# Tiles, latents and weights in two shared buffers, one transpose per tile, and a dense layer in two parts

## The chip, the cores and the metric

The kernel runs on one core of one Trainium2 chip. The metric is the device time of one execution in microseconds (us): the median of several runs of the same program. The core has five engines that work beside each other, each through its own instructions in order: TensorE (PE) multiplies matrices and adds into eight banks of PSUM; VectorE (DVE), ScalarE (ACT) and GpSimd (POOL) work element by element, POOL on SBUF only; SyncE (SP) issues transfers, among them the transposes by DMA. Engines wait for each other by semaphores only.

## The reference, cut to what matters

Two layers over x of shape (2, 1024, 512), two batches of 1024 tokens:

```python
xn = layernorm(x)
x = x + attn0(xn) + streams0(xn)      # one head of 128; four streams mixed by a Sinkhorn matrix
xn = layernorm(x)
x = x + attn1(xn) + ffn1(xn)

# attn1: 32 causal query heads of 128, 8 key/value heads out of latents
lat = concat(xn @ Wk_down.T, xn @ Wv_down.T, per head)   # 512 columns
k, v = (first half of lat) @ Wk_up.T, (second half) @ Wv_up.T
out = softmax(q @ k.T * scale + causal) @ v, then @ Wo.T

# ffn1: a dense layer and a low-rank part weighted by a gate
gates = relu(layernorm(xn @ gw1.T + gb1)) @ gw2.T + gb2
top 2 of 8 experts, softmax of the two -> top_g
allowed = (tokens of each expert, over BOTH batches, <= capacity)
w = top_g where allowed, else 0                          # combine weights
out = xn @ weight.T + ((xn @ lora_A) * w) @ lora_B / 16
```

The combine weights of batch 0 need the gates of batch 1 too, since tokens are counted over both.

## The kernel before

Every fp32 operand of a product is split into two fp16 parts, high and low, and a product is three passes (high-high, high-low, low-high), added up in PSUM; `mm3` (line 84) does that. A weight is loaded in fp32 and split by three POOL instructions (`split_pool`, line 93: scale, cast, subtract). A product is brought out of PSUM by `evac` (line 104): ACT writes the high part, DVE the low part.

A tile is 128 tokens; a batch has eight. `normed_T` (line 228) makes a tile of xn for the products: it scales the tile (on DVE, POOL or ACT), casts it (ACT), subtracts (DVE or POOL) and has SP transpose both parts by DMA into a destination. `layernorm_tiles` (line 215) makes the statistics on DVE.

After layer 0 (lines 996 to 1049) layer 1 runs as one loop over 16 groups of four query heads, eight groups per batch, each of 32 steps (`layer1_attn`, line 785). A step computes the scores of 32 query rows of four heads against the keys so far (`row_step`, line 339), the softmax of the step before, and the transposes of its probabilities. A step at the start of a group is short and one at its end is long, since the attention is causal. All else hangs on steps: `at` and `put` enter a function at a step (an absolute number, 32 per group), and it is called when the loop comes there. So group 6 is steps 192 to 223, group 7, the last of batch 0, is 224 to 255, and group 14 is 448 to 479. What is entered:

- for the next group: keys and values (`kv`, line 712: load, split, two key products, two value products), query products, output weights
- for the group itself: probabilities times values (`av`), the output product (`wo_block`, line 751), which adds to the residual `acc` and, in a batch's last group, sends the tile out
- for batch 1's layer 0: Sinkhorn on POOL (steps 1 to 116), mixing (122 to 193)
- batch 1's second layer norm in one piece, `late_norm` (step LN1 = 198)
- gating: `gating_h` (the product with gw1) and the steps of `gating` (line 893, DVE throughout); batch 0 from step G0 = 16, batch 1 from G1 = 200
- `weights_of` (line 943) at WT = 220: one product with ones counts the experts' tokens over both batches, DVE makes the combine weights of both
- the dense layer of batch 0: `ffn_fetch` and `ffn_split` for six 256 KB weights (A to D dense, E and F low-rank) from FW = 210, `ffn_block` (line 975) from FF = 221; of batch 1 from step 464 and 483
- batch 1's tiles from LX = 231, its latents from LA = 240, its first keys from step 243

The scheduler that builds the program simulates it and orders each engine's instructions by what is ready, so functions of neighbouring steps mix.

Two buffers of 16 KB per partition hold the large things. `xT` (one buffer) holds the transposed tiles: layer 0 of batch 0, of batch 1, then layer 1 of batch 0 and of batch 1. `cmp` (one buffer) holds layer 0's weights, batch 0's latents, its six dense weights, batch 1's latents, its dense weights. Batch 1's tiles can't enter `xT` before batch 0's dense layer and last query products have read it (step 231), but its gating is needed before. So `tile_of` (line 1033) makes each of batch 1's tiles a first time, into a small buffer, for the gating alone (steps 200 to 207), and `xT_tile` makes it again at step 231 and later.

`ffn_block` computes the low-rank product (128 columns), multiplies it by the combine weights (`tw`, DVE), splits it (`twhl`, two DVE instructions), transposes it (`twT`, SP), and adds dense and low-rank products in one PSUM bank: 12 matmuls with A to D, then 3 with `twT` and F. PSUM has three banks for such products (`pp`), four for scores, one for `av`.

Of the kernel before, what the change touches and what calls it, by code (L numbers as in the profile page):

```python
# [9 lines left out]
F16 = mybir.dt.float16  # L10
F32 = mybir.dt.float32
AF = mybir.ActivationFunctionType
# [4 lines left out]
P = 128  # L17
S = 1024
NB = 2
NT = S // P  # L20
H = 512
NC = H // P
NH = 32
NG = 8
# [4 lines left out]
FB, PB, LB, XB, WB = 4, 3, 3, 4, 9  # L29
# [9 lines left out]
CA, CB, CC, CD = 4, 1, 1, 3  # L39
SK0, SKN, MX0, MXN, LN1 = 1, 116, 122, 74, 198  # L40

G0, G1, GL, WT, LX, LA = 16, 200, 3, 220, 231, 240
AVD, WOD = 5, 10
KVN, QN, QNN, QH = 19, 18, 24, 1
MG = range(8, 16)
FW, FF = 210, 221
BS, BP, BV = 4, 3, 1
CQ, CV = (0, 1), (0, 0)
PSCALE = 16384.0
# [3 lines left out]
def tile_model(ctx: ExitStack, tc: tile.TileContext, out: bass.AP, a: dict):  # L53
# [30 lines left out]
    def mm3(dst, pairs):  # L84

        n = len(pairs)
        for i, (lhs, rhs) in enumerate(pairs):
            for j, (l, r) in enumerate(PASSES):
                nc.tensor.matmul(dst, lhs(l), rhs(r),  # L89
                                 start=(i == 0 and j == 0),  # L90
                                 stop=(i == n - 1 and j == 2))
# [37 lines left out]


    load_x(0)
    w0 = T("cmp", [P, NC * 2 * S], F16, bufs=1)
    cut = [0]

    def part0(*shape):
# [79 lines left out]
    def layernorm_tiles(b, mv, rs, ts):  # L215
        ve = T("ve", [P, NT], bufs=2)
        sl = slice(ts[0], ts[-1] + 1)
        for t in ts:
            st = T("bnst", [P, 6], bufs=2)
            V.bn_stats(st, acc[b, t])  # L220
            V.bn_aggr(mv[:, t, :], st)
# [3 lines left out]
        return V.scalar_tensor_tensor(rs[:, 1, sl], mv[:, sl, 0], -1.0, rs[:, 2, sl],  # L225
                                      ALU.mult, ALU.mult)

    def normed_T(b, mv, rs, t, dst, pool, tags=(("f2k", FB), ("wo", WB))):

# [140 lines left out]

    def front0(b, between=lambda: None):
        mv, rs = layernorm(b, "a")
        xT = T("xT", [P, NT, 2 * NC, P], F16, bufs=1)
        for ts in F0[b]:
            layernorm_tiles(b, mv, rs, ts)
            for t in ts:
# [311 lines left out]
                last_lat[0] = evac(src, dst[:, :, 0, :], dst[:, :, 1, :], 0.125)  # L688

    def latents(b):  # L690
        cmp[b] = T("cmp", [P, NC, 2, S], F16, bufs=1)

    def lat_w(mc):
        st = T("f2k", [P, NC, P], bufs=FB)
# [51 lines left out]
    def qproj(b, w, Q, hh, half):  # L746

        p = proj_T(lambda c, l: w[:, l, c, :], xT1[b], half)
        evac(p.rearrange("p (b q) -> p b q", q=QR), Q[:, 0, :, hh, :], Q[:, 1, :, hh, :], 0.125)

    def wo_block(b, t, ao, wos, last):
        p = PP()
        mm3(p, [(lambda l, h=h: ao[:, l, h, :],
                 lambda r, h=h: wos[h][:, r, :]) for h in range(4)])
        V.scalar_tensor_tensor(acc[b, t], p, 1.0 / 256.0, acc[b, t], ALU.mult, ALU.add)  # L755
        if last:
            nc.scalar.dma_start(out[(b * NT + t) * P:(b * NT + t + 1) * P, :], acc[b, t])

    def group_av(Vh, Vm, PT, c, k, p):

# [24 lines left out]
    def layer1_attn(kv0, start, extra):  # L785
# [43 lines left out]
        for g in range(N):  # L829
            if g + 1 < N:  # L830
                new = (g + 1) % NG == 0
                kvs[g + 1], fs = kv((g + 1) // NG, (g + 1) % NG)
                at(g, KVN - 2 if new else 1, fs[0])
                for k, f in enumerate(fs[1:]):
                    at(g, KVN + 2 * k if new else 1 + 4 * k + 2 * (k == 0), f)
                for hh in range(4):
                    at(g, 5 + 4 * hh, lambda g=g, hh=hh: fetch_q(g + 1, hh))
                    at(g, 7 + 4 * hh, lambda g=g, hh=hh: split_q(g + 1, hh))
                for u in range(4):
                    at(g, QNN + 2 * u if new else QN + 4 * u, lambda g=g, u=u: q_unit(g + 1, u))  # L840
# [124 lines left out]
    def ffn_fetch(k):  # L965
        ffw[k] = fetch(ffw_parts[k][0])

    def ffn_split(k):
        if k == 0:
            ffw["w"] = T("cmp", [P, 6, 2, H], F16, bufs=1)  # L970
        w = ffw["w"][:, k]
        behind(split_pool(ffw[k], w[:, 0], w[:, 1], ffw_parts[k][1]), last_low[0], True)
        ffw["ABCDEF"[k]] = w

    def ffn_block(b, t):
        xT = xT1[b]
        pa = PP()
        la = ffw["E"].rearrange("p l (c d) -> p l c d", c=NC)
        mm3(pa[:, :P], [(lambda l, c=c: xT[:, t, 2 * c + l, :],
                         lambda r, c=c: la[:, r, c, :]) for c in range(NC)])  # L980
        tw = T("tw", [P, 8, 16], bufs=1)
        V.scalar_tensor_tensor(tw, pa[:, :P].rearrange("p (e r) -> p e r", r=16), 1.0 / 16.0,
                               bc(wts[b][:, t, :], 2, 16), ALU.mult, ALU.mult)
# [3 lines left out]
        nc.sync.dma_start_transpose(tT, hl.rearrange("p l d -> p (l d)"))  # L987
        p = PP()
        mm3(p, [(lambda l, c=c: xT[:, t, 2 * c + l, :],
                 lambda r, c=c: ffw["ABCD"[c]][:, r, :]) for c in range(NC)]  # L990
            + [(lambda l: tT[:, l, :], lambda r: ffw["F"][:, r, :])])
        V.scalar_tensor_tensor(acc[b, t], p, 1.0 / 256.0, acc[b, t], ALU.mult, ALU.add)


    f0, ln1 = {}, {}
# [28 lines left out]
    adv(200)  # L1024

    def new_xT(b):
        xT1[b] = T("xT", [P, NT, 2 * NC, P], F16, bufs=1)
# [34 lines left out]
    gw1 = gating_w()  # L1062
    chain = sinkhorn(1, logit[1])

    def late_norm():
        ln1[1] = layernorm(1, "b")
        layernorm_tiles(1, *ln1[1], range(NT))
# [19 lines left out]
    hs, gates, dts, lw = {}, {}, {}, {}  # L1087

    def gate_start(b):
        hs[b] = T("xr", [P, NT, 32], bufs=XB)  # L1090
# [17 lines left out]
    put(0, LX, lambda: new_xT(1))  # L1108
    for t in range(NT):
# [9 lines left out]
        for th in range(2):  # L1119
            put(0, LA + 2 * mc + th, lambda mc=mc, th=th: lat_unit(mc, th))  # L1120
    for k in range(6):
        for s in (FW, 8 * 58 + 2):
            put(0, s + 2 * k - 2, lambda k=k: ffn_fetch(k))
            put(0, s + 2 * k, lambda k=k: ffn_split(k))
# [51 lines left out]
```

## Time and profile before

| what | value |
|---|---|
| median of 3 runs | 1851.71 us (1848.24 to 1853.01) |
| the profiled execution: span from first to last instruction | 1846.2 us |
| instructions | 35059 |
| PE busy | 1708.2 us, 93% |
| DVE busy | 1473.1 us, 80% |
| ACT busy | 1191.1 us, 65% |
| POOL busy | 896.5 us, 49% |
| mean granted PE clock | 0.976 of full speed |

The execution that was profiled has no time of its own beside its span; the runs are others of the same program. The page's slices of the span, 46.2 us each, show where engines work, in tenths:

```profile
PE   4666389999999999998999999999999999999998
DVE  8888968988888878778976768778787877787675
POOL 5568629778766465647634433323242424235200
PEclk9888699999999999999999999999999999999999
```

A 9 stands for 90% or more. Layer 0 takes the first six slices, with gaps on PE; layer 1 fills the rest. The slices 18 to 22 (counted from 0, from 831 to 1062 us) are where batch 0 ends and batch 1 begins: there PE has its one 8 between slice 5 and the last, and DVE a 9 (slice 19). A matmul counts as busy from its start to a modelled end, so a busy PE isn't always PE at its peak.

### The profile page before, as it was taken

The page shows a single profiled execution, that of the slowest core. Times are in us where ns is not written, and L with a number is a line of the kernel's source. Part 1 is how long each engine was busy: PE and PEld are TensorE (multiplying, and loading weights), DVE is VectorE, ACT ScalarE, POOL GpSimd, SP SyncE. Part 2 cuts the span into 40 slices and gives each one's busy share as a digit, 9 for nine tenths or more (in the row PEclk, how much of TensorE's full clock was granted, in tenths as well). Part 3 has the DMA queues.
Part 4 walks back from the last instruction along what each step waited for, and adds up shares of the span by engine and source line. Part 5 has one row for each costly group of instructions (what it writes and reads, how often), then busy time and mean ns, then how long its engine had stood idle before and what let it go on. Part 6 is the DMA issues. An engine that isn't in the chain of part 4 may idle for free.

```text
span 1846.2 us, 35059 instructions
## 1 busy us (share of the span) xinstructions
PE 1708.2 (93%) x11394; PEld 1038.5 (56%) x11394; DVE 1473.1 (80%) x4162; ACT 1191.1 (65%) x2917; POOL 896.5 (49%) x1476
## 2 busy tenths in 40 slices
PE   4666389999999999998999999999999999999998
PEld 2434146566666566655555566666666666666565
DVE  8888968988888878778976768778787877787675
ACT  4848666656676778876544656667666767676564
POOL 5568629778766465647634433323242424235200
PEclk9888699999999999999999999999999999999999
DMA  7435225656575656468645656556566655566455
GB/s 212 82 56 132 59 44 123 151 118 139 119 149 98 141 128 144 105 142 143 146 98 125 144 126 140 135 124 141 125 134 124 142 118 142 124 143 135 97 121 118
DMA packets 693482, 230.25 MB, mean 125 GB/s; under 512 B 674081, under 2 KB 674209, under 8 KB 693298
## 3 DMA queue, kind: packets, MB, share of 16 engines
q1 hardware_dynamic: 677842, 180.75, 47.3%
q0 software_dynamic: 13152, 43.07, 8.7%
q10 hardware_dynamic: 2304, 4.20, 0.7%
q8 instruction: 89, 1.46, 0.3%
q14 instruction: 95, 0.78, 0.1%
HBM read 52.81 MB, written 4.19 MB: 31 GB/s over the span
## 4 chain that ended last, share of the span: by engine, by line
PE 47%; DVE 2%; DMA 1%; POOL 1%; issue 1%; ACT 0%; SPq 0%; DVEq 0%
PE pp L89 26%; PE av L365 11%; PE s L89 10%; DVE Phl L330 0%; DVE f2k L913 0%; DMA f2k<-in_Wq 0%; DMA xT<-wo 0%; DVE P L288 0%; POOL wo L241 0%; DMA PT<-Phl 0%; POOL f2k L95 0%; SPq L335 0%; DVE P L284 0%; DMA twT<-twhl 0%; DVE Q L106 0%
## 5 line engine op out<-in xcount | busy, mean ns | idle before, releaser
L292 ACT ACTIVATE P<-P,nm 128x1024 f32<-128x1024 f32 (+31 forms) x528 | 391.5, 742 | 280.9 <-DVE nm L284 263.4
L330 DVE SCALAR_TENSOR_TENSOR Phl<-P,r,Phl 128x64 f16<-128x64 f32 (+16 forms) x627 | 460.8, 759 | 75.7 <-ACT Phl L322 70.3
L89 PE MATMUL s<-K,Q 128*128 128x512 f16 (+22 forms) x2400 | 439.1, 317 | 19.7 <-DVE P L288 11.7
L365 PE MATMUL av<-PT,V 128*128 128x256 f16 x3456 | 425.6, 274 | 9.4 <-DMA PT<-Phl 8.5
L365 PEld LDWEIGHTS <-V 128*128 128x128 f16 x3456 | 338.2, 98 | 92.9 <-DMA PT<-Phl 10.6
L322 ACT ACTIVATE Phl<-P,r 128x1024 f16<-128x1024 f32 (+31 forms) x515 | 369.5, 730 | 20.6 <-DMA PT<-Phl 5.3
L89 PE MATMUL pp<-xT,wq 128*128 128x512 f16 x1536 | 371.8, 381 | 4.5 <-DVE Q L106 2.3
L89 PE MATMUL pp<-wo,ao 128*128 128x512 f16 x1536 | 369.9, 379 | 2.0 <-ACT ao L105 1.9
L95 POOL TENSOR_SCALAR f2k<-f2k 128x512 f32<-128x512 f32 x164 | 113.9, 695 | 500.6 <-DVE Phl L330 458.9
L89 PEld LDWEIGHTS <-Q 128*128 128x128 f16 x2400 | 222.8, 98 | 175.7 <-issue 27.7
L89 PEld LDWEIGHTS <-wq 128*128 128x128 f16 x1536 | 149.7, 98 | 172.6 <-issue 6.8
L89 PEld LDWEIGHTS <-ao 128*128 128x128 f16 x1536 | 149.5, 98 | 156.9 <-ACT ao L105 3.4
L284 DVE CUSTOM_DVE_ANT_0 P<-s,mask,nm 128x272 f32<-128x272 f32 (+15 forms) x256 | 157.3, 615 | 9.3 <-PE s L89 1.0
L288 DVE TENSOR_SCALAR_CACHE_REDUCE P<-s 128x512 f32<-128x512 f32 (+15 forms) x272 | 152.6, 562 | 13.4 <-PE s L89 11.2
L316 DVE RECIPROCAL r<-r 128x1 f32<-128x1 f32 x528 | 78.9, 154 | 87.5 <-ACT P L292 84.5
L317 ACT ACTIVATE r<-r 128x1 f32<-128x1 f32 x528 | 95.6, 192 | 60.2 <-DVE r L316 59.7
L105 ACT ACTIVATE ao<-av 128x512 f16<-128x512 f32 x128 | 74.9, 585 | 81.7 <-PE av L365 81.5
L334 POOL MEMSET Phl<- 128x192 f16 (+1 forms) x320 | 56.2, 189 | 142.3 <-DMA PT<-Phl 97.3
L105 ACT ACTIVATE Q<-pp 128x512 f16<-128x512 f32 x128 | 74.6, 583 | 64.3 <-PE pp L89 60.0
L284 DVE CUSTOM_DVE_ANT_0 P<-s,mask 128x32 f32<-128x32 f32 (+15 forms) x256 | 103.7, 430 | 14.9 <-PE s L89 14.2
L755 DVE SCALAR_TENSOR_TENSOR acc<-pp,acc 128x512 f32<-128x512 f32 x128 | 87.1, 681 | 35.1 <-PE pp L89 34.7
L106 DVE SCALAR_TENSOR_TENSOR Q<-pp,Q 128x512 f16<-128x512 f32 x128 | 87.4, 683 | 34.0 <-ACT Q L105 33.7
(256 smaller groups left out, 2153.1 us busy)
## 6 DMA issues: line engine op xcount, KB each, us to landing
f2k<-in_Wq POOLq DMA_DIRECT2D x64, 256.0 KB, 3.1
f2k<-in_WoT POOLq DMA_DIRECT2D x64, 256.0 KB, 3.3
PT<-Phl SPq DMA_TRANSPOSE x528, 3.2
acc<-in_x SPq DMA_DIRECT2D x16, 256.0 KB, 5.1
f2k<-in_Wup POOLq DMA_DIRECT2D x16, 256.0 KB, 3.3
out<-acc ACTq DMA_DIRECT2D x16, 256.0 KB, 3.5
xr<-V SPq DMA_DIRECT2D x32, 128.0 KB, 2.4
xr<-in_x SPq DMA_DIRECT2D x12, 256.0 KB, 3.9
```

The costliest lines, as they stand in the source:

```text
L89: nc.tensor.matmul(dst, lhs(l), rhs(r), start=(i == 0 and j == 0), stop=(i == n - 1 and j == 2))
L95: first = G.tensor_scalar(stage, stage, scale, 1.0, ALU.mult, ALU.mult)
L105: A.activation(hl_hi, src, AF.Copy, scale=scale)
L106: return V.scalar_tensor_tensor(hl_lo, src, scale, hl_hi, ALU.mult, ALU.subtract)
L284: last_row[0] = V.tensor_tensor_reduce(Pm[:, o:o + w], pt[:, :w], mask[:, 512 - w:], -scale, first, ALU.add, ALU.min, nm[:, k:k + 1])
L288: last_row[0] = V.tensor_scalar(Pm[:, o:o + w], pt[:, :w], -scale, first, ALU.mult, ALU.min, accum_out=nm[:, k:k + 1])
L292: A.activation(Pm[:, :W], Pm[:, :W], AF.Exp, bias=last, scale=-1.0, accum_out=r[:, 0:1])
L317: A.activation(r[:, 1:2], r[:, 1:2], AF.Copy, scale=PSCALE)
L322: A.activation(hl[1], Pm[:, :W], AF.Copy, scale=r[:, 1:2])
L330: last_low[0] = V.scalar_tensor_tensor(lo, Pm[:, a0:a1], r[:, 1:2], hi[:, a0:a1], ALU.mult, ALU.subtract)
L365: nc.tensor.matmul(p, v, pt, start=(k == 0), stop=(k == len(todo) - 1))
L755: V.scalar_tensor_tensor(acc[b, t], p, 1.0 / 256.0, acc[b, t], ALU.mult, ALU.add)
```

## The change

- `cmp` and `xT` become one tag, `big`, with two buffers of the same 16 KB. A new tile takes whichever is free.
- Batch 1's tiles are made once, into a `big` buffer, at steps LX = 217 and on; `tile_of` is gone, and `gating_h` of batch 1 reads these tiles three steps later.
- For that a buffer must be free while batch 0's tiles live. Keys and values of a batch's last group are computed earlier (KVL: steps 3, 4, 5, 7 and 8 of the group before it, not 3, 5, 9, 13 and 17; groups 6 and 14), so that the latents can go; then A to E take their buffer from step 201, and batch 1's tiles take it after them.
- Batch 0's dense layer is cut in two around the combine weights, which now come at WT = 240. `ffn_first` (from FF = 209): the low-rank product goes to an fp32 tile of its own (`lows`, by ACT), and the 12 dense matmuls are added to `acc`. `ffn_rest` (from LF = 241): the combine weights are put to the kept product, and the 3 matmuls with F, split apart into an `xr` buffer, are added to `acc` by a second DVE addition. Batch 1 keeps `ffn_block` as one piece.
- Batch 1's gating steps move from 211 to 228 and on, its latents from 240 to 232.
- The statistics of batch 1's second norm are spread over steps 198 to 205, the rest of it at 206.
- A tile of batch 0 leaves when both its output product of group 7 and `ffn_rest` are through (`missing`, `store`).

```diff
-G0, G1, GL, WT, LX, LA = 16, 200, 3, 220, 231, 240
+G0, G1, GL, WT, LX, LA = 16, 217, 3, 240, 217, 232
+LF = 241
+KVL = (3, 4, 5, 7, 8)
-FW, FF = 210, 221
+FW, FF = 201, 209
...
-    w0 = T("cmp", [P, NC * 2 * S], F16, bufs=1)
+    w0 = T("big", [P, NC * 2 * S], F16, bufs=2)
...
+    missing = {(0, t): 2 for t in range(NT)}
+    def store(b, t):
+        missing[b, t] = missing.get((b, t), 1) - 1
+        if missing[b, t] == 0:
+            nc.scalar.dma_start(out[(b * NT + t) * P:(b * NT + t + 1) * P, :], acc[b, t])
...
+                last = (g + 2) % NG == 0
                 for k, f in enumerate(fs[1:]):
-                    at(g, KVN + 2 * k if new else 1 + 4 * k + 2 * (k == 0), f)
+                    at(g, KVN + 2 * k if new else KVL[k] if last else 1 + 4 * k + 2 * (k == 0), f)
...
-    def ffn_split(k):
-        if k == 0:
-            ffw["w"] = T("cmp", [P, 6, 2, H], F16, bufs=1)
-        w = ffw["w"][:, k]
+    def ffn_split(k, apart=False):
+        if apart:
+            w = T("xr", [P, 2, H], F16, bufs=XB)
+        else:
+            if k == 0:
+                ffw["w"] = T("big", [P, 6, 2, H], F16, bufs=2)
+            w = ffw["w"][:, k]
...
+    def ffn_first(b, t):
+        lows[t] = T("ysum", [P, P], bufs=8)
+        A.activation(lows[t], ffn_low(b, t), AF.Copy, scale=1.0 / 16.0)
+        ffn_add(b, t, ffn_main(b, t))
+    def ffn_rest(b, t):
+        ffn_add(b, t, ffn_weigh(b, t, lows[t], 1.0))
+        store(b, t)
+    def ffn_block(b, t):
+        low = ffn_weigh(b, t, ffn_low(b, t), 1.0 / 16.0)
+        ffn_add(b, t, ffn_main(b, t) + low)
...
-    def tile_of(b, t):
-        d = T("wo", [P, 2 * NC, P], F16, bufs=WB)
-        normed_T(b, *ln1[b], t, d, True, (("f2k", FB), ("xr", XB)))
-        return d
...
-            if b == 0:
-                put(0, s + t, lambda t=t: gating_h(hs[0], t, gw1, xT1[0][:, t]))
-            else:
-                put(0, s + t, lambda t=t: dts.update({t: tile_of(1, t)}))
-                put(0, s + t + GL, lambda t=t: gating_h(hs[1], t, gw1, dts[t]))
+            put(0, s + t + GL * b, lambda b=b, t=t: gating_h(hs[b], t, gw1, xT1[b][:, t]))
...
-    put(0, LN1, late_norm)
+    for t in range(NT):
+        put(0, LN1 + t, lambda t=t: late_stats(t))
+    put(0, LN1 + NT, late_norm)
...
+        if k < 5:
+            put(0, FW + 2 * k - 2, lambda k=k: ffn_fetch(k))
+            put(0, FW + 2 * k, lambda k=k: ffn_split(k))
+    put(0, LF - 4, lambda: ffn_fetch(5))
+    put(0, LF - 2, lambda: ffn_split(5, True))
     for t in range(NT):
-        put(0, FF + t, lambda t=t: ffn_block(0, t))
+        put(0, FF + t, lambda t=t: ffn_first(0, t))
+        put(0, LF + t, lambda t=t: ffn_rest(0, t))
         put(60, 4 * t + 3, lambda t=t: ffn_block(1, t))
```

The new functions it calls: `ffn_low` is the low-rank product of a tile into PSUM; `ffn_weigh` puts the combine weights to it, splits and transposes it, and returns the pair of `twT` and F; `ffn_main` returns the four pairs of A to D; `ffn_add` multiplies what it is given and adds it to `acc`. `late_stats` makes one tile's statistics, `late_norm` the rest of the norm.

More of the change, by code (lines that the diff above doesn't have):

```diff
@@ L213, in layernorm, with norm_stats, norm_scales @@
         return mv, rs
-    def layernorm_tiles(b, mv, rs, ts):
+    def norm_stats(b, mv, t):
+        st = T("bnst", [P, 6], bufs=2)
+        V.bn_stats(st, acc[b, t])
+        V.bn_aggr(mv[:, t, :], st)
+    def norm_scales(mv, rs, ts):
         ve = T("ve", [P, NT], bufs=2)
         sl = slice(ts[0], ts[-1] + 1)
[L218 to L221, printed above, removed]
         V.tensor_scalar(ve[:, sl], mv[:, sl, 1], LN_EPS, None, ALU.add)
@@ L226, in layernorm_tiles @@
                                       ALU.mult, ALU.mult)
+    def layernorm_tiles(b, mv, rs, ts):
+        for t in ts:
+            norm_stats(b, mv, t)
+        return norm_scales(mv, rs, ts)
     def normed_T(b, mv, rs, t, dst, pool, tags=(("f2k", FB), ("wo", WB))):
@@ L372, in front0 @@
         mv, rs = layernorm(b, "a")
-        xT = T("xT", [P, NT, 2 * NC, P], F16, bufs=1)
+        xT = T("big", [P, NT, 2 * NC, P], F16, bufs=2)
         for ts in F0[b]:
@@ L690, in latents @@
     def latents(b):
-        cmp[b] = T("cmp", [P, NC, 2, S], F16, bufs=1)
+        cmp[b] = T("big", [P, NC, 2, S], F16, bufs=2)
     def lat_w(mc):
@@ L756, in wo_block @@
         if last:
-            nc.scalar.dma_start(out[(b * NT + t) * P:(b * NT + t + 1) * P, :], acc[b, t])
+            store(b, t)
     def group_av(Vh, Vm, PT, c, k, p):
@@ L966, in ffn_fetch, with ffn_low @@
         ffw[k] = fetch(ffw_parts[k][0])
-    def ffn_split(k):
-        if k == 0:
-            ffw["w"] = T("cmp", [P, 6, 2, H], F16, bufs=1)
-        w = ffw["w"][:, k]
+    def ffn_split(k, apart=False):
[5 more added lines that the diff above has]
+            w = ffw["w"][:, k]
         behind(split_pool(ffw[k], w[:, 0], w[:, 1], ffw_parts[k][1]), last_low[0], True)
         ffw["ABCDEF"[k]] = w
-    def ffn_block(b, t):
+    def ffn_low(b, t):
         xT = xT1[b]
@@ L980, in ffn_block, with ffn_weigh @@
                          lambda r, c=c: la[:, r, c, :]) for c in range(NC)])
+        return pa[:, :P]
+    def ffn_weigh(b, t, low, scale):
         tw = T("tw", [P, 8, 16], bufs=1)
-        V.scalar_tensor_tensor(tw, pa[:, :P].rearrange("p (e r) -> p e r", r=16), 1.0 / 16.0,
+        V.scalar_tensor_tensor(tw, low.rearrange("p (e r) -> p e r", r=16), scale,
                                bc(wts[b][:, t, :], 2, 16), ALU.mult, ALU.mult)
@@ L987, in ffn_block, with ffn_main, ffn_add @@
         nc.sync.dma_start_transpose(tT, hl.rearrange("p l d -> p (l d)"))
+        return [(lambda l: tT[:, l, :], lambda r: ffw["F"][:, r, :])]
+    def ffn_main(b, t):
+        return [(lambda l, c=c: xT1[b][:, t, 2 * c + l, :],
+                 lambda r, c=c: ffw["ABCD"[c]][:, r, :]) for c in range(NC)]
+    def ffn_add(b, t, pairs):
         p = PP()
-        mm3(p, [(lambda l, c=c: xT[:, t, 2 * c + l, :],
-                 lambda r, c=c: ffw["ABCD"[c]][:, r, :]) for c in range(NC)]
-            + [(lambda l: tT[:, l, :], lambda r: ffw["F"][:, r, :])])
+        mm3(p, pairs)
         V.scalar_tensor_tensor(acc[b, t], p, 1.0 / 256.0, acc[b, t], ALU.mult, ALU.add)
+    lows = {}
+    def ffn_first(b, t):
[4 more added lines that the diff above has]
+        ffn_add(b, t, ffn_weigh(b, t, lows[t], 1.0))
+        store(b, t)
+    def ffn_block(b, t):
+        low = ffn_weigh(b, t, ffn_low(b, t), 1.0 / 16.0)
+        ffn_add(b, t, ffn_main(b, t) + low)
     f0, ln1 = {}, {}
@@ L1026, in new_xT @@
     def new_xT(b):
-        xT1[b] = T("xT", [P, NT, 2 * NC, P], F16, bufs=1)
+        xT1[b] = T("big", [P, NT, 2 * NC, P], F16, bufs=2)
     def xT_tile(b, t, pool):
@@ L1063, in tile_model, with late_stats @@
     chain = sinkhorn(1, logit[1])
+    def late_stats(t):
+        if t == 0:
+            ln1[1] = layernorm(1, "b")
+        norm_stats(1, ln1[1][0], t)
     def late_norm():
-        ln1[1] = layernorm(1, "b")
-        layernorm_tiles(1, *ln1[1], range(NT))
+        norm_scales(*ln1[1], range(NT))
     extra = {}
@@ L1086, in tile_model @@
         put(1, 2 * t, lambda t=t: branch0_add(1, t, y4s[t], f0[1][4]))
-    hs, gates, dts, lw = {}, {}, {}, {}
+    hs, gates, lw = {}, {}, {}
     def gate_start(b):
@@ L1121, in tile_model @@
     for k in range(6):
-        for s in (FW, 8 * 58 + 2):
-            put(0, s + 2 * k - 2, lambda k=k: ffn_fetch(k))
-            put(0, s + 2 * k, lambda k=k: ffn_split(k))
+        if k < 5:
+            put(0, FW + 2 * k - 2, lambda k=k: ffn_fetch(k))
+            put(0, FW + 2 * k, lambda k=k: ffn_split(k))
+        put(58, 2 * k, lambda k=k: ffn_fetch(k))
+        put(58, 2 * k + 2, lambda k=k: ffn_split(k))
+    put(0, LF - 4, lambda: ffn_fetch(5))
+    put(0, LF - 2, lambda: ffn_split(5, True))
     for t in range(NT):
-        put(0, FF + t, lambda t=t: ffn_block(0, t))
+        put(0, FF + t, lambda t=t: ffn_first(0, t))
+        put(0, LF + t, lambda t=t: ffn_rest(0, t))
         put(60, 4 * t + 3, lambda t=t: ffn_block(1, t))
```

## The prediction

> **What bounds the kernel now.** I read the chain of waits first, then the busy time by group, then TensorE's (PE's) waits and the rows around them.
>
> ```profile
> PE 47%; DVE 2%; DMA 1%; POOL 1%; issue 1%; ACT 0%; SPq 0%; DVEq 0%
> ```
>
> The chain that ended last can be followed back to 893 us, and 47% of the span on PE is 868 of the 953 us behind that: from there on PE is the bound. The groups of layer 1 begin where the first 32-column score product appears; over four of them (5 to 8, numbered from 0):
>
> ```profile
> core 0: us, PE busy (x) PEld busy (x) DVE busy (x) ACT busy (x) POOL busy (x), PEclk, DMA share, GB/s
> 729.00:825.79 96.79, 95.66 (x630) 58.50 (x628) 75.41 (x201) 76.60 (x209) 55.89 (x81) 1.00 0.59 128
> 825.79:946.92 121.13, 108.32 (x784) 67.25 (x782) 103.72 (x277) 72.56 (x175) 82.17 (x116) 0.96 0.72 147
> 946.92:1086.15 139.23, 137.16 (x861) 78.22 (x862) 95.66 (x250) 75.54 (x183) 48.84 (x76) 1.00 0.54 123
> 1086.15:1177.40 91.25, 91.25 (x608) 56.41 (x606) 72.53 (x202) 60.79 (x149) 31.58 (x51) 1.00 0.58 133
> ```
>
> Columns: length, then PE, weight loads, VectorE (DVE), ScalarE (ACT) and GpSimd (POOL) with counts, granted clock, DMA. Group 6 is the sick one: DVE 86% and POOL 68% busy, PE not full, clock 0.96. How much is lost there follows from PE's timeline, where matmuls in a run start 0.216 us apart at 512 columns (12 in 2.59), 0.109 at 256, 0.056 at 128, 0.025 at 32. Group 6 holds 207, 261, 72 and 96 of these, and 144 score products whose widths add up to 21.5: 44.7 + 28.5 + 4.0 + 2.4 + 21.5 = 101.1 (101.2 with the two tiny ones). Group 7: 405 of 512 columns, 192 of 256, 120 of 128 and the scores, 136.6. The same sum gives groups 8 to 14 their measured lengths within 0.1, so PE has no slack there. Loss: 121.1 - 101.2 = **19.9 us in group 6, 139.2 - 136.6 = 2.6 in group 7**. Groups 1 to 5 lose 5.6, 1.4, 0.9, 1.6 and 3.5.
>
> ```profile
> 858.19 0.81 PE L89 MATMUL s<-K,Q 128*128 128x512 f16 x3
> 861.22 4.44 PE L89 MATMUL pp<-xT,wq 128*128 128x512 f16 x12 [2.22 <-DVE acc L755]
> ```
>
> ```profile
> 850.04 3.41 DVE L330 SCALAR_TENSOR_TENSOR Phl<-P,r,Phl 128x352 f16<-128x352 f32 x1
> 850.79 2.27 POOL L241 TENSOR_TENSOR xr<-f2k,xr 128x512 f16<-128x512 f32 x2
> ```
>
> PE waits 2.22 us for a DVE addition and then runs its 12 matmuls in 4.44 us, not 2.75. Ten microseconds before, a DVE low part that takes 0.82 at this width on average, this one counted in, took 3.41, beside two subtractions of batch 1's first set of tiles on POOL. Mapped onto PE's work, the 19.9 lie as 10.4 before 869 us and 9.5 between 914 and 947, where the gating of batch 1 fills DVE and the two count products and the first low-rank product follow it:
>
> ```profile
> PE pp L946 <- DVE ch L940: 1.1, 1, 1.1
> PE pp L89 <- DVE al L948: 0.7, 1, 0.7
> ```
>
> **The change, part by part.** PE runs 11394 matmuls in both; the dense layer's 15 wide products per tile are only cut into 12 and 3. So the time moves only by what PE waits, and 22.5 us is all that groups 6 and 7 have to give. In the changed order they hold 118.8 and 120.2 us of matmuls.
>
> *Shared buffers.* Layer 0's order differs only in neighbours changing places (first weights split after, not before, four scale steps). Two loads of 16 KB stay live, as before. PE is idle 107 us before 276 us, 70 of them for transposed tiles, which hang on the loads, the norms and a serial chain of 0.3 us steps on DVE; no neighbour changes their number, and a swap costs or gives a DVE row or two. I take 0, -2 to +2.
>
> *First set of tiles gone.* Removed: 8 scalings (1.01) and 8 subtractions (1.19) on POOL, 17.7 us; 8 casts on ACT (0.62), 5.0; 8 transposes on SP (issue to landing 3.8). None is on PE's path by itself; they lengthen DVE's rows and fill queues. POOL in group 6 falls from 82 to about 62 us (its last dense weight, 3.0 us of three rows, leaves too), a load near groups 4 and 5, which lose 1.6 and 3.5. The first 10.4 us become 4 (1 to 6).
>
> The Trainium skill, "SBUF — State Buffer", section "Who interferes with whom", says that a DVE instruction with two SBUF inputs and a POOL instruction that reads SBUF exclude each other for a whole instruction; the 3.41 us row agrees. By it up to 17.7 us of DVE time would come back, this part would fall to 0 and the sum below to -10.5 (1841.2). The same rule speaks against the change where POOL splits the dense weights in one run: were DVE blocked through all of it, the next part would be 8.7 in place of 2, and the sum +0.2 (1851.9).
>
> *Dense weights earlier, products in group 6.* Buffer, weights and first product form a queue: last value product of group 7; on POOL four casts and four subtractions in a row (4 x 0.77 + 4 x 1.41 = 8.7), since four weights wait for the latents' buffer; four DMA issues (4 x 0.58); a query weight's three rows (2.6); then cast and subtraction of the fifth weight (2.2): about 16 us, against some 15 us of PE work in the changed order until PE wants that weight. Behind that product on PE stand scores, and behind these the softmax rows. Cost 0 to 8.7 (all of the run of eight); I take 2. Eight ACT copies of 128 columns (0.28) replace the casts. Eight more additions on DVE (0.61 each in a run, 4.9 us) come where 17 us of gating leave (8 x 0.70, 8 x 0.41, some 8 of small rows), covered by PE. The 9.5 us go; 2 stay.
>
> *Buffer handed on twice more.* Batch 1's eight transposes go into the dense weights' buffer, so the first waits on SP for the eighth main product, and the softmax transposes behind it wait too. Some 10 us of PE work stand between that product and the first gating product that reads the tiles, against a landing of 3.3; latents need the old tiles' buffer, free after group 7's last query product, with 5 us of PE work before the first eviction. Both 0; if SP's queue eats the cover, one landing, inside the upper bound of the next part.
>
> *Gating, latents, combine weights in group 7.* Before, DVE was busy 95.7 there; with the gating it needs about 113 of PE's 120. They bunch: from the 9th to the 29th score row the changed order puts 56.7 us of matmuls on PE, and on DVE 32 score reductions (18.1), 19 low parts (15.5), 32 latent lows (11.3), 12 evictions (7.4), gating (7.7), combine weights (1.2), their products' splits (3.3), 21 reciprocals (1.8): 66.3, each row at its listed mean less the 0.07 by which consecutive rows overlap. DVE is short by 9.6. In group 6 the same count between the 17th and the 29th row was 38.7 against 30.7, short by 8, and PE lost 9.5. So I take 10 in place of 2.6; from 2.6 (four score banks and spare work at the group's end take the lag up) to 18 (all of the gating's 17 beside the old loss).
>
> *Low-rank product alone.* Three matmuls per tile now wait for a chain of three DVE rows, a transpose (landing 2.3) and SP's queue, without their own tile's 12 matmuls before them. The order gives the chain some 4 us of DVE rows between the last split and the addition that reads the product; before, 16 such blocks made PE wait 0.2. Behind a late product stand scores and output products on PE, and DVE's rows wait for these. I take 0; rival B prices the rest. Both norm parts and earlier key and value work in groups 6 and 14 move DVE rows of equal number; group 14 loses 0.0 and its like, groups 8 to 10, have DVE 78 to 80% busy, so 0.
>
> Sum: 4 + 2 + 10 = 16 in place of 22.5, **-6.5 us**. The profiled span is 1846.2, the median 1851.7 (5.5 above, for what lies around the span and the spread of runs); the span falls to 1839.7 and the median to **1845.2**. Bounds of the parts: 1 + 0 + 2.6 - 2 = 1.6 and 6 + 8.7 + 18 + 2 = 34.7, that is -20.9 and +12.2.
>
> **Rivals.**
>
> A, no change: gating merely brings its loss to group 7 (12) and the early loss stays, since group 1's 5.6 shows that POOL needs no such tiles for it (6), with 4 on the weights: 22, 1851. For it: DVE's total grows. Against: 17.7 us of POOL leave the worst place.
>
> B, slower: the three matmuls stand at PE's head until their transpose lands. SP's queue waited 16.1 us in 5 cases for these splits, once 7.6, and softmax transposes now stand between. If PE waits 2.3 (one landing) for each of 8, that is 18.4: 1863. From 0.8 each (6.5 / 8) the gain is lost. Against: the wait of 0.2 in 16 blocks, spread over less crowded DVE queues though.
>
> C, better: DVE's lag is taken up and both losses shrink to the average of groups 1 to 5 (2.6 each): 22.5 - 5.2 = 17.3, 1834. For it: 14 us of spare PE work follow in group 7. Against: PE keeps its order, and group 6 lost all that DVE was short.
>
> **How the numbers follow.** Forecast 0.45 (1840 to 1850), C 0.17, A 0.23, B 0.15. The range must reach A and part of B and C: 1833 to 1859 leaves out some 0.1 on each side. 0.3% (5.6 us) is about what a measurement can tell from no change: faster means below 1846.1, slower above 1857.3. Faster 0.17 + 0.31 of the forecast's 0.45 + 0.02 of A = 0.50; slower 0.13 of B and 0.03 of A = 0.16; the rest 0.34.
>
> **What would show it.** Group 6 near 125 us (118.8 + 6) with no DVE low part above 3 us in its first half; a PE wait for the fifth dense weight's POOL rows of 0 to 3 us; group 7 near 130 with DVE above 90% in its middle and PE waiting there for DVE rows; groups 8 to 14 unchanged. Wrong if PE waits repeatedly for the combine transposes (B), if group 7 has no PE wait (C), or if time up to 270 us moves by more than 2.

## The result, and the profile after

The changed kernel takes 1865.1 us (median of 6 runs, 1861.9 to 1870.0) against 1852.4 for the kernel before (6 runs beside them): ratio 1.0073, 95% interval 1.0056 to 1.0090. It is slower by some 13 us (12.7 between the medians, 13.5 by the ratio), where -6.5 was forecast. The profiled spans are 1861.8 and 1846.2, a difference of 15.6.

First the chain that ended last, and the slices of the span, from the page of the changed kernel:

```profile
PE 40%; DVE 2%; DMA 1%; issue 1%; ACT 0%; SPq 0%; DVEq 0%; ACTq 0%; POOL 0%; POOLq 0%
```

```profile
PE   4766389999999999999999799999999999999998
DVE  7988968988888877778579847878787877777675
```

The slices are 46.5 us each. PE's share of the chain has gone from 47% (868 us) to 40% (745 us): the stretch before the end in which PE's own work sets the pace is shorter. PE's weak slice inside layer 1 is slice 22, a 7 (counted from 0: 1024 to 1070 us), late in group 7; DVE has a 9 just before it, an 8 in it and a 4 behind it.

Where the 15.6 us lie follows from the first 32-column score of each group, read off PE's timeline in both traces:

| stretch | before | after | difference |
|---|---|---|---|
| up to group 0 | 263.7 | 266.9 | +3.2 |
| groups 0 to 5 | 562.1 | 562.1 | 0.0 |
| group 6 | 121.1 | 126.3 | +5.2 |
| group 7 | 139.2 | 145.5 | +6.3 |
| groups 8 and 9 | 183.2 | 182.1 | -1.1 |
| groups 10 to 13 | 363.7 | 363.7 | 0.0 |
| group 14 to the last output product | 206.2 | 208.4 | +2.2 |

Set against PE's matmuls, which the change moves between groups, group 6 loses 126.3 - 118.8 = 7.5 and group 7 145.5 - 120.2 = 25.3; together 32.8 in place of 22.5. The two groups in windows (columns as in the prediction):

```profile
829.00:955.30 126.30, 120.14 (x863) 73.50 (x862) 88.39 (x218) 70.31 (x173) 61.16 (x91) 1.00 0.60 118
955.30:1100.80 145.50, 128.75 (x796) 72.46 (x794) 115.71 (x320) 79.96 (x189) 54.06 (x90) 0.95 0.59 129
```

Group 6 is better, as forecast: DVE at 70% in place of 86%, the clock at 1.00, 126.3 us. The larger loss is now in group 7, with the granted clock down to 0.95. What PE waits for there, in total, times and longest:

```profile
PE s L91 <- DVE P L296: 6.8, 5, 4.2
PE pp L91 <- DMA twT<-twhl: 3.9, 4, 3.0
PE pp L91 <- DVE big L108: 3.5, 1, 3.5
PE av L373 <- DVE r L324: 1.2, 1, 1.2
PE av L373 <- DVE ao L108: 0.8, 1, 0.8
PE pp L91 <- DVE acc L770: 0.6, 1, 0.6
```

16.8 us of waits; the other 8.5 are, for the most part, slow matmuls behind them. By this view alone DVE's rows (12.9) would be the cause and the transposes of the combine weights (`twT`, 3.9) a side matter. Their own rows say more. One tile's chain, from DVE, SP and PE:

```profile
1055.69 0.28 DVE L1004 SCALAR_TENSOR_TENSOR tw<-ysum,wt 128x128 f32<-128x128 f32 x1
1058.14 1.18 DVE L103 TENSOR_SCALAR twhl<-tw 128x128 f16<-128x128 f32 x1
1062.11 0.44 DVE L104 SCALAR_TENSOR_TENSOR twhl<-tw,twhl 128x128 f16<-128x128 f32 x1
```

```profile
1063.07 1.17 SPq L1009 DMA_TRANSPOSE twT<-twhl  x1
```

```profile
1067.07 1.46 PE L91 MATMUL pp<-xr,twT 128*128 128x512 f16 x3 [3.00 <-DMA twT<-twhl]
1068.32 5.09 PE L91 MATMUL pp<-wo,ao 128*128 128x512 f16 x12
```

Three rows that usually take 0.2 to 0.3 us each lie 7.4 us apart from first start to the transpose: softmax rows of up to 1.1 us stand between them on DVE, and the cast (1058.14) can't write `twhl` before the transpose of the tile before has landed (PE's product on it starts at 1057.60). The transpose takes 4.0 to reach PE; and PE, which stood 3.00 us, then needs 1.46 for three matmuls and 5.09 for twelve, where 0.81 and 2.75 are usual for such rows. The eight low-rank products start on average 6.8 us apart (1032.6 to 1080.1), while the order puts 31.5 us of matmuls between the first and the last, 4.5 each. Here alone 16.0 us are lost. Whether the chain or DVE's fullness is to blame needs experiments.

### The profile page after: what moved, and what is told of

Read it like the earlier page. It is cut to its first block, busy times and chain, and to the rows that moved or that the text cites. A ratio compares the mean times of both kernels' runs of the same rounds, so it can differ in the third digit from the quotient of the medians.

```text
span 1861.8 us, 35011 instructions
## 1 busy us (share of the span) xinstructions
PE 1711.8 (92%) x11394; PEld 1038.0 (56%) x11394; DVE 1476.4 (79%) x4170; ACT 1193.1 (64%) x2917; POOL 875.0 (47%) x1460
## 3 DMA queue, kind: packets, MB, share of 16 engines
q8 instruction: 89, 1.46, 0.3%
## 5 line engine op out<-in xcount | busy, mean ns | idle before, releaser
L373 PE MATMUL av<-PT,V 128*128 128x256 f16 x3456 | 423.9, 274 | 11.5 <-DMA PT<-Phl 8.1
L91 PE MATMUL pp<-big,wq 128*128 128x512 f16 x1536 | 370.1, 382 | 5.7 <-DVE big L108 3.2
L91 PEld LDWEIGHTS <-big 128*128 128x128 f16 x1824 | 120.9, 99 | 86.7 <-DMA big<-wo 41.1
L91 PE MATMUL pp<-big,big 128*128 128x128 f16 (+2 forms) x816 | 103.7, 283 | 16.7 <-DMA big<-wo 16.5
```

The source lines that it names most:

```text
L91: nc.tensor.matmul(dst, lhs(l), rhs(r), start=(i == 0 and j == 0), stop=(i == n - 1 and j == 2))
L373: nc.tensor.matmul(p, v, pt, start=(k == 0), stop=(k == len(todo) - 1))
```

## The experiments

In what follows "the rest" is the time from group 6's first score to the start of the last output product's final run of matmuls, and "the entry" that from layer 1's first 512-column product to group 0's first score. The rest without any loss would be 1013.5 - 22.5 - 1.4 = 989.6 (before's, less its losses in groups 6, 7 and 15). Ratios are to the kernel before on the same chip.

| kernel | ratio (interval) | entry | group 7 | rest |
|---|---|---|---|---|
| before, two profiles | | 40.2, 36.9 | 139.2, 142.2 | 1013.5, 1016.6 |
| changed | 1.0073 (1.0056 to 1.0090) | 43.6 | 145.5 | 1025.9 |
| changed, again | 1.0086 (1.0059 to 1.0113) | 42.2 | 146.6 | 1028.8 |
| constant tile | 1.0016 (1.0003 to 1.0028) | 43.9 | 129.1 | 1012.2 |
| more buffers | 1.0008 (0.9996 to 1.0020) | 42.1 | 133.8 | 1014.5 |
| four tiles at a time | 1.0014 (1.0002 to 1.0025) | 44.2 | 135.0 | 1017.9 |
| two steps each | 1.0030 (1.0014 to 1.0047) | 41.9 | 135.4 | 1017.6 |
| eight steps later | 1.0033 (1.0021 to 1.0045) | 44.0 | 137.4 | 1019.2 |
| gating moved away | 1.0067 (1.0046 to 1.0089) | 43.8 | 135.3 | 1016.5 |
| group 14 as before | 1.0058 (1.0039 to 1.0076) | 42.2 | 144.2 | 1022.4 |
| entry as before | 1.0077 (1.0050 to 1.0103) | 37.5 | 144.8 | 1024.5 |
| entry as before, again | 1.0069 (1.0049 to 1.0090) | 40.8 | 145.3 | 1026.4 |

**The chain taken out.** Batch 0's low-rank product reads a tile of ones; all rows and transposes are still issued.

```diff
-        return [(lambda l: tT[:, l, :], lambda r: ffw["F"][:, r, :])]
+        return [(lambda l: tT[:, l, :] if b else ones, lambda r: ffw["F"][:, r, :])]
```

> The changed kernel, but batch 0's low-rank products read a constant tile of ones in place of the transposed low-rank values, so that no product of batch 0 waits for a transpose; the rows on DVE and the transposes on SP are all still issued, and each addition still follows its product. Theory 'DVE is short': PE's 3.9 us of waits for transposes turn into waits for DVE's rows, group 7 still loses 20 or more, and the time is 1860 to 1866. Rival 'the products that stand alone wait for their transposes': with the slow matmuls behind the waits 7 us or more go, and what hangs on them too: group 7 loses 18 or less, 1857 or less.

Group 7 falls to 129.1, the rest by 13.7 (16.5 against the second profile of the changed kernel), and the clock in group 7 is 1.00 again. PE's waits there:

```profile
PE pp L91 <- DVE big L108: 4.1, 2, 3.5
PE pp L91 <- DVE acc L1019: 1.3, 2, 0.7
PE pp L91 <- DVE K L108: 1.0, 1, 1.0
```

The largest waits for DVE's rows, 6.8 us in 5 cases, are gone with the waits for the transposes, though DVE has the same rows to do. So they go with the chain; by what way is not shown. The longest of them, 4.2 us, ended at 1038.1 in the changed kernel, when transposes had held PE for only 0.2 us, so it did not follow from PE standing at a product; ahead of it on DVE stood the second tile's split and the first product's addition, among softmax rows. The rival holds, "DVE is short" falls as the main cause. It isn't empty: the 3.5 us wait stays. But the scheduler also moved the eight products forward, as nothing held them: the first comes behind 61.1 us of group 7's matmuls in place of 67.9, the last behind 83.3 in place of 99.4. This run alone doesn't tell the dependence from the order; the next one does better.

**More buffers.** The split and the transposed tile of batch 0 take the weights' nine buffers in place of one each.

```diff
-        hl = T("twhl", [P, 2, P], F16, bufs=1)
+        hl = T("twhl", [P, 2, P], F16, bufs=1) if b else T("wo", [P, 2, P], F16, bufs=WB)
-        tT = T("twT", [P, 2, P], F16, bufs=1)
+        tT = T("twT", [P, 2, P], F16, bufs=1) if b else T("wo", [P, 2, P], F16, bufs=WB)
```

> The changed kernel, but the split and the transposed values of batch 0's low-rank part take their buffers from the nine that the weights use, so that a tile needn't wait until the tile before has been transposed and multiplied. Theory 'the single buffers hold the chain up': groups 6 to the end take 1016 to 1020 in place of 1026 to 1029, ratio 1.001 to 1.004. Rival 'the rows are late on DVE and the transposes on SP's queue, whatever the buffers': DVE's waits for these buffers (2.3 us) go and little else, 1023 or more, ratio 1.006 to 1.009.

The rest is 1014.5, better than expected, with every row, transpose and product in place. PE's two largest waits in group 7 and the one for the chain, and two of the low-rank products:

```profile
PE pp L91 <- DVE big L108: 3.5, 1, 3.5
PE s L91 <- DVE P L296: 3.0, 3, 1.9
PE pp L91 <- DMA wo<-wo: 0.2, 1, 0.2
```

```profile
1033.88 0.82 PE L91 MATMUL pp<-xr,wo 128*128 128x512 f16 x3 [0.18 <-DMA wo<-wo]
1067.70 0.81 PE L91 MATMUL pp<-xr,wo 128*128 128x512 f16 x3
```

These are the first and the eighth: 33.8 us apart in place of 47.5, with 0.2 us of waits for the chain's transposes in all. PE's order is nearly that of the changed kernel: the first product comes behind 67.9 us of group 7's matmuls in both, the last behind 97.9 in place of 99.4. Between the two PE loses 3.8 us in place of 16.0. So the chain was held by its single buffers, `twhl` above all: a tile's split couldn't start until the transpose before had read it. In the changed kernel all seven later splits began 0.02 to 1.1 us after that transpose had landed, two of them with DVE standing idle for it:

```profile
1041.51 0.23 DVE L103 TENSOR_SCALAR twhl<-tw 128x128 f16<-128x128 f32 x1 [1.63 <-DMA twT<-twhl]
1067.11 0.23 DVE L103 TENSOR_SCALAR twhl<-tw 128x128 f16<-128x128 f32 x1 [0.65 <-DMA twT<-twhl]
```

With more buffers five of these seven splits begin before that landing. The order of DVE's rows changes with the buffers too; how much of the gain is waiting and how much is that order isn't told apart.

**Fewer, larger steps.** The combine weights for four tiles at a time: 12 DVE rows in place of 24, two transposes in place of eight, products four steps behind.

```diff
+        hl = T("xr", [P, 4, 2, P], F16, bufs=XB)
+        split_dve(tw.rearrange("p t e r -> p t (e r)"), hl[:, :, 0, :], hl[:, :, 1, :], 1.0)
+        tT4[q] = T("wo", [P, 8, P], F16, bufs=WB)
+        nc.sync.dma_start_transpose(tT4[q], hl.rearrange("p t l d -> p (t l d)"))
...
+            put(0, LF + t // 2, lambda t=t: ffn_weigh4(0, t // 4))
+        put(0, LF + 4 + t, lambda t=t: ffn_rest(0, t))
```

> The changed kernel, but batch 0's combine weights are applied to four tiles at a time: eight rows for the weighting, two casts, two subtractions (12 rows on DVE in place of 24) and two transposes on SP in place of eight, at steps 241 and 243; the eight products follow at steps 245 to 252. Theory 'the chain of weighting, split, transpose and product, one tile after the other through single buffers, holds PE up': groups 6 to 9 lose about 18 us in place of 32.7, as with the constant tile, no wait of PE for a transpose is above 1 us, and the ratio to before is 1.000 to 1.003 (1851 to 1857). Rival 'DVE is short': only some 3 us of its rows go, 29 or more are lost, ratio 1.005 to 1.007.

The ratio is in the first theory's range, and the rest falls by 8.0. But that is less than expected: one wait for a transpose was left, 3.2 us at the first product, and groups 6 to 9 lose 25.0 us against their own matmuls (19.2 with the constant tile, counted in the same way), not 18.

**The same chain with more time, or elsewhere.**

```diff
-        put(0, LF + t, lambda t=t: ffn_rest(0, t))
+        put(0, LF + 2 * t, lambda t=t: ffn_rest(0, t))
```

> The changed kernel, but batch 0's combine and low-rank products have two steps each (241, 243, to 255) in place of one. Theory 'the chain takes longer than the one step that PE's order gives it': the waits for transposes fall below 1 us in all, groups 6 to 9 lose 18 to 22 in place of 32.7, ratio 1.000 to 1.003. Rival 'each product waits for its own transpose however far apart they stand': four or more waits, 28 or more lost, ratio 1.005 or more.

PE's waits for the chain's transposes are 0.2 us in all and the rest falls by 8.3, as the first theory has it, though groups 6 to 9 still lose 24.3, not 18 to 22. What is left in group 7 are waits for the transposed probabilities (3.9), for the latents' rows on DVE (3.5) and for softmax rows (2.7). The other way, `LF = 249` in place of 241:

> The changed kernel, but batch 0's combine and low-rank products start 8 steps later (249 to 256 in place of 241 to 248), past the gating and the latents, where DVE is 30% to 45% busy in the changed kernel. Theory 'DVE is short in the middle': groups 6 to 9 lose 16 to 20 in place of 32.7, ratio 1.000 to 1.003. Rival 'the chain through single buffers takes 5 to 7 us for each tile wherever it stands': PE waits for the transposes as before, 26 or more are lost, ratio 1.004 to 1.007.

Measured, group 7 into group 8 of the later kernel:

```profile
PE pp L91 <- DMA twT<-twhl: 6.4, 4, 3.0
```

Four waits, more than before: the rival is right about the waits. But the rest fell by 6.8, in between: PE's waits for softmax rows on DVE in group 7, 6.8 us in the changed kernel, are down to 0.4. Neither account alone carries this run.

**Gating out of group 7.** Batch 1's gating reads batch 0's tiles, from step 80 on.

```diff
-    for b, s in ((0, G0), (1, G1)):
+    for b, s in ((0, G0), (1, G0 + 64)):
...
-            put(0, s + t + GL * b, lambda b=b, t=t: gating_h(hs[b], t, gw1, xT1[b][:, t]))
+            put(0, s + t + GL * b, lambda b=b, t=t: gating_h(hs[b], t, gw1, xT1[0][:, t]))
```

> The changed kernel, but batch 1's gating is computed from batch 0's tiles and 64 steps after batch 0's own, in group 2, so that its 17 us of DVE rows are not in group 7; the combine weights are those of batch 0 for both batches. Theory 'DVE is short in the middle of group 7 because the gating meets the latents and the combine weights there': the loss of group 7 falls from 25.3 to 8 or less, and the time to 1848 (1845 to 1852). Rival 'the chain from the combine weights through the transposes on SP's queue': that chain stays, the loss stays at 18 to 22, and the time is 1858 to 1862.

Group 7 takes 135.3 with 118.9 us of matmuls (of the 2.4 us that moved, 1.2 were in group 6), so it still loses 16.4, between the two and nearer to the rival. The waits that remain there:

```profile
PE pp L91 <- DMA twT<-twhl: 7.4, 3, 3.6
PE s L91 <- DVE nm L292: 1.7, 2, 1.0
PE s L91 <- DVE P L296: 0.6, 1, 0.6
```

With DVE busy for 101 us in place of 116, PE waits longer for the transposes than before. Most of the 8.9 us won here was paid elsewhere: groups 0 to 5 took 568.8 in place of 562.1 (2.4 of it the matmuls that moved there; 561.9 to 565.5 in all other profiles), and group 6 lost 1.5 more.

**Group 14.** Keys and values where they stood, for group 14 alone (`KVL[k] if last and g < NG else`).

> The changed kernel, but group 14 has its keys' and values' steps where they stood before (spread over the group); group 6 keeps the early ones. Theory 'the early steps cost groups 14 and 15 the 2.3 us': their losses fall from 3.7 to about 1.4 and the time from 1865.1 to about 1862.8. Rival 'the loss comes from the dense weights or products of batch 1, which stand elsewhere': groups 14 and 15 lose 3 to 4 as now, 1865.

From group 14 on 206.2, the value of before, in place of 208.4: by the profile the early steps cost the 2.2 us. The ratio, 1.0058, has an interval that overlaps with the changed kernel's.

**The entry.** In the trace of before ScalarE's (ACT's) second step of the inverse square root follows the first at once; in the changed kernel an eviction of the latents stands between, and DVE waits for it. ACT before, then ACT and DVE of the changed kernel:

```profile
226.53 0.20 ACT L202 ACTIVATE rs<-ve 128x4 f32<-128x4 f32 x1 [6.25 <-DVE ve L222]
226.76 0.20 ACT L203 ACTIVATE rsb<-rs 128x4 f32<-128x4 f32 x1
```

```profile
226.51 0.20 ACT L204 ACTIVATE rs<-ve 128x4 f32<-128x4 f32 x1 [6.23 <-DVE ve L225]
227.66 0.38 ACT L107 ACTIVATE big<-pp 64x256 f16<-64x256 f32 x1 [0.95 <-PE pp L91]
227.94 0.19 ACT L205 ACTIVATE rsb<-rs 128x4 f32<-128x4 f32 x1
```

```profile
228.07 0.42 DVE L108 SCALAR_TENSOR_TENSOR big<-pp,big 64x256 f16<-64x256 f32 x1 [1.60 <-ACT big L107]
```

Four tiles' norms, transposes and latents come later by that, PE waits twice in place of once, and 48 matmuls run in 13.4 us in place of 10.5.

```diff
+            with after(last_exp[0], *(last_rs[1:] if mc == 0 else ())):
+                lat_evac(0, mc, 0, p)
```

> The changed kernel, but the first evictions of batch 0's latents are kept behind the second step of the inverse square root on ACT (and the first block's low parts behind the last scale row on DVE), as they stood before the change. Nothing else is changed. Theory 'an order that swapped at the entry of layer 1 costs the 3.2 us': the first 32-column score starts at 263.7 to 264.4 us in place of 266.9, and the time falls from 1865.1 to about 1862. Rival 'the shared buffers themselves hold something up': the start stays at 266 to 267, and the time at 1865.

> The kernel with only the entry's old order (first evictions of the latents behind the inverse square root), once more with more runs. Theory 'the entry costs 3 to 4 us': ratio 1.0045 to 1.0065 (the changed kernel has 1.0073 and 1.0086). Rival 'the entry isn't in the time': 1.007 to 1.009. In the profile the stretch from layer 1's first 512-column product to its first 32-column score takes 37 to 41 us by the first, 42 to 44 by the second.

Both profiles have a short entry (37.5, 40.8), but the ratios, 1.0077 and 1.0069, don't differ from the changed kernel's. The kernels before and after, once more, show why a single pair of profiles says little here:

> The kernel before, unchanged, for a second profile: does the entry of layer 1 move from one execution to the next? Theory 'the entry scatters': its first 32-column score stands at 261 to 269 us and more than 1.5 us away from 263.7, while group 6 to the end takes 1013.5 within 1 us. Rival 'the entry is fixed by the order': within 1 us of 263.7.

> The changed kernel, unchanged, once more. Theory 'the entry scatters': its first 32-column score stands more than 1.5 us away from 266.9, while group 6 to the end takes 1026 within 1.5 us; ratio 1.006 to 1.009. Rival: the entry within 1 us of 266.9.

Group 0 began at 261.8 and 270.2, where the first pair had 263.7 and 266.9: each kernel scatters by 2 to 3 us. The rest moved by 3 as well (1016.6 and 1028.8), more than expected. Over all profiles the entry takes 41.4 to 44.2 in the new order (eleven, mean 42.9), 36.9 and 40.2 in before and 37.5 to 41.2 with the order put back (four, mean 40.1). Some 3 us are there in profiles; in unprofiled runs they are not shown for this edit alone.

**Versions put together.**

> The changed kernel with the combine weights applied to four tiles at a time, the entry of layer 1 in the old order (first eviction of the latents behind the inverse square root) and group 14's keys and values where they stood. If the three losses are separate (chain 14, entry 3 to 6, group 14 2.2), the time is 1865 - 19 to 1865 - 22, 1843 to 1846 (ratio 0.996 to 0.998). If the entry's gain is not there in unprofiled runs (the entry alone gave 1863.8 in place of 1865.1), 1847 to 1850 (ratio 0.998 to 1.000). If the chain's loss is not cured by this, above 1855.

1.0010 (0.9998 to 1.0023), rest 1015.8, entry 41.2: better than the changed kernel, not than before, and above both of the first two forecasts.

> The changed kernel with group 14's keys and values in their old places, batch 1's latents two steps apart (232 to 246), and batch 0's combine and low-rank products two steps apart from step 249 on (249 to 263). If what is left of the loss in group 7 is DVE's shortage where gating and latents meet (a wait of 3.5 us and its slow matmuls, 5 in all) and the chain, group 6 to the end takes 1026 - 2.2 - 8.3 - 5 = 1010.5, and the ratio is 0.997 to 0.999. Rival 'what is moved out of group 7 is paid in group 8': 1014 or more, ratio 1.000 or more.

1.0029 (1.0016 to 1.0042): group 7 is down to 123.7, but groups 8 and 9 take 194.2 in place of 182.1, 2.7 of it matmuls that moved there and 9.4 lost in group 8. The rival: it was paid in group 8.

> As the kernel with two steps for each product, but with the combine weights applied to four tiles at a time at steps 249 and 251, and the products at 253 to 260. Theory 'chain and shortage are both gone': group 6 to the end takes 1008 to 1012, ratio 0.996 to 0.999. Rival as there: 1014 or more, ratio 1.000 or more.

0.9980 (0.9964 to 0.9997), rest 1009.6, as its first theory has it: a little faster than before. With the entry's old order as well:

> The kernel with four tiles' combine weights at a time from step 249, latents two steps apart and group 14's old steps (ratio 0.998), with the entry's old order as well. Theory 'the entry costs 3 to 4 us': ratio 0.995 to 0.997. Rival: 0.997 to 0.999.

**0.9952 (0.9934 to 0.9971), 1844.0 against 1852.0 us: faster than both kernels.** Group 7 of this version:

```profile
956.80:1081.10 124.30, 116.70 (x769) 68.56 (x768) 107.07 (x300) 77.09 (x185) 49.08 (x84) 1.00 0.64 138
```

The clock is at 1.00, and no wait there is above 2.5 us. Against the version without the entry's order the intervals overlap by a hair, so the entry's share isn't settled.

## Why the prediction was wrong

By the profiled pair, the sum went like this:

| step of the prediction | forecast | measured |
|---|---|---|
| shared buffers, up to group 0 | 0 | +3.2 (scatter 2 to 3) |
| first set of tiles gone (early loss of group 6) | 10.4 to 4 | 19.9 to 7.5 for this line and the next |
| dense weights earlier (late loss of group 6) | 9.5 to 2 | |
| gating, latents, combine weights bunch | 2.6 to 10 | 2.6 to 11.5 |
| low-rank product alone | 0 | +13.7 |
| keys and values in group 14 | 0 | +2.2 |
| sum | -6.5 | +15.6 |

Where a line has two numbers, they are the loss before and after. The 11.5 is the constant tile's rest (1012.2) less 989.6, less 7.5 in group 6 and less 3.6 from group 14 on (before's 1.4 and the 2.2); the 13.7 is the fall to that rest. So 3.2 + (7.5 + 11.5 - 22.5) + 13.7 + 2.2 = 15.6, which is 22.1 above the forecast; 13.7 of it is one step.

- **The step that failed is "Low-rank product alone ... I take 0".** It argued from 16 blocks in which PE had waited 0.2 us, and saw that the 12 matmuls ahead were gone and that DVE was more crowded, but it counted "some 4 us of DVE rows" for one tile and never asked how often the chain can run. With one buffer for `twhl` and one for `twT`, a tile's split waits for the last transpose; the cycle became 6.8 us, against 4.5 us of PE work per tile in the order. With more buffers the rest falls by 11.4, with the dependence gone by 13.7. Rival B, with 0.15, had the place: it needed 0.8 us per tile to decide, and the constant tile gives 1.7 (13.7 / 8). That its time, 1863, is so near to 1865.1 is in part luck: it took eight waits of 2.3 us, 18.4, and nothing for the entry and group 14, where PE waited four times, 3.9 in all, the chain cost 13.7, and those two added 5.4. The prediction's own sign of rival B, repeated waits for the combine transposes, was there. The waits at the transposes are thus the smaller part of the chain's cost; the rest lies in waits for DVE's rows that go away with it, and in matmuls at a lower clock.
- **Group 6 was right**: forecast near 125, measured 126.3. No DVE low part of its first half is above 3 us: the longest took 2.43 (96 columns), where before had one of 3.41. Against "a PE wait for the fifth dense weight of 0 to 3 us", there was none. Its parts were less right than their sum: the early part lost some 7 (forecast 4, at most 6), the late one next to nothing (forecast 2).
- **The bunching was right in mechanism and size**: 10 forecast, 11.5 measured without the chain, and moving the gating away took 8.9 off group 7's loss with the chain left in. DVE was 94% busy from 975 to 1065 us, above 90% as forecast, and 38% behind 1075. With the chain left out the kernel would have been at +1.9 by the same terms, still not at -6.5.
- **Two zeros were small losses in the profiled pair**, together 5.4: the entry, forecast at 0 with 2 either way, where each kernel scatters by 2 to 3, and group 14, where "DVE 78 to 80% busy, so 0" was wrong. Why the early keys and values cost 2.2 there wasn't looked into.

## What to carry to other kernels

When a dependent product is cut off from the work that stood ahead of it, cost its chain as a loop, not as one passage: the buffers of every link, the time from link to link in the queues as they will be, and the PE work that the order gives per turn. PE's waits list the last releaser only; a run that takes one dependence away and leaves all work in place shows what a chain costs in full, here 13.7 us for 3.9 listed, as long as the order of the rest is compared too (with more buffers and nearly the same order on PE it was 11.4). DVE had a fifth of group 7 to spare and the chain still ran late through it. More buffers won nearly as much as taking the dependence away, while moving the gating was paid for in other groups; so look at buffers before you move work.

## What the runs showed of the hardware

- After a wait PE pays again. In the changed kernel 12 matmuls took 5.09 us soon behind a wait of 3.00, in place of 2.75, with a granted clock of 0.54 over these 5.09 us (0.50 from 1066.2 to 1073.0); in the trace of before 12 took 4.44 behind a wait of 2.22, at 0.62. The Trainium skill, "TensorE: Matmul & The Clock Gate", section "What's actually happening", has two clocks, one half of the other, and the lower one after an idle window of about 3.4 us that runs free. The halving agrees. But here waits shorter than that were enough: in the 3.4 us before the clock fell PE was busy for 0.8 us in the changed kernel and for 1.2 in the one before.
- DVE rows beside POOL's subtractions: in the changed kernel, with two subtractions on POOL at 1033.6 and 1035.1,

```profile
1034.07 1.23 DVE L104 SCALAR_TENSOR_TENSOR twhl<-tw,twhl 128x128 f16<-128x128 f32 x1
1035.22 1.80 DVE L338 SCALAR_TENSOR_TENSOR Phl<-P,r,Phl 128x672 f16<-128x672 f32 x1
```

  The first usually takes 0.29 (median of 16), and a wider neighbour of the second, at 704 columns, 0.94. PE's longest wait, 4.2 us, ended with the rows behind these. What would be left of it without POOL's subtractions was not tried, so this part of group 7's loss may be POOL's as well as the chain's.
- Groups 10 to 13 took 363.7 us in sixteen of seventeen profiles (364.3 in one), while the start of layer 1's first wide product scattered from 221.8 to 228.0. Where PE is the bound the time repeats to a tenth; where it waits for chains it does not.
